# Another way of turning the third graph's normed x, and another order of work under the first graph's attention

## The chip, the core and the metric

The kernel runs on one core of a Trainium2 chip. The metric is the time of one execution on the device in microseconds (us), as the median of several runs. The core has five engines that run side by side, each in its own order of instructions: TensorE (PE, matrix products and transposes), VectorE (DVE), ScalarE (ACT), GpSimd (POOL) and SyncE (SP). SP and POOL issue the transfers (DMAs) of this kernel. An engine waits for another, or for a transfer, through semaphores. All numbers are float32.

## The reference, cut to what matters

There are 16 graphs (b) with 1024 nodes (n) and 256 channels (c), one adjacency matrix for all of them, and two layers. Each layer adds its result to x.

```python
# layer 0: graph attention
h = maximum(layernorm(x), 0)                  # (16, 1024, 256), "normed x"
fea = transpose(h, (0, 2, 1))
c_adj = mean(fea, axis=1)                     # mean over channels
diff = c_adj[:, None, :] - c_adj[:, :, None]
A = abs(abs(sigmoid(diff) - 0.5) - 0.5) * 2
Wg = adj * (A + A.transpose(0, 2, 1)) * 0.5   # weights of each graph
g = relu(einsum('bcn,bnm->bcm', fea, Wg) * para)
q = heads(transpose(g))                       # 4 heads of 64 channels
k, v = heads(h @ kv_w)
x = x + softmax(q k^T * scale) v
# layer 1: graph convolution with batch norms
h = maximum(layernorm(x), 0)
A_norm = adj + eye
deg = column sums + row sums - diagonal of A_norm
A_hat = A_norm * rsqrt(deg)[:, None] * rsqrt(deg)[None, :]
agg = einsum('nm,bmd->bnd', A_hat, h)
x = x + batchnorm(relu(batchnorm(agg @ W1.T + b1)) @ W2.T + b2)
```

## The kernel before, in words

**Steps and background.** `attention()` (L1240) goes through 16 steps for each graph: 2 pairs of heads, 2 halves of the queries, 4 groups of keys. In a step PE makes two tiles of scores (`scores`, L1071), ACT takes their exponentials (L1089), DVE adds these up (L1113), and PE multiplies the exponentials of the step before with the values (L1124). The scores live in two PSUM buffers (`ps_sc`), so the scores of a step start only when ACT has done the exponentials of the step before.

Between the steps lies other work, made by the generator `background(b)` (L964): it prepares the next graphs and finishes earlier ones. Each `yield` names a cost in us of PE's time. `attention` hands out pieces while the costs handed out are below the share that is due, `total * (step + 1) / 16`. A piece of cost 0 comes along with its neighbours. A piece that yields `TOP` runs at the top of the next step, ahead of the values' product. `weave(main, (start, side), ...)` takes one piece of each side after every piece of the main generator, from the `start`-th on. Each engine runs its instructions in the order in which this Python code issues them; nothing is rescheduled.

**What lies under the first graph's attention** (`background(0)`, L966 to L997):

- `transposed(1, (k,))` (L412) turns the second graph's normed x, one half of its channels at a time: 8 transposes on PE (L424) and 2 copies on ACT (L430) from PSUM into a tile `ht`. Keys and values need x turned in this way.
- `keys_values(1)` (L672): 4 pieces of keys (`pk`), 4 pieces of values (`pv`), each of 1.71.
- `plain_queries(1)` (L638): 16 pieces (`pg`), eight for each half of the nodes. The two sums of a half stay in two of the three PSUM banks of `bank()` until DVE has multiplied them with `para` (L663).
- `weighers[1]`, made by `weigh` (L477): 17 slots for eight weight tiles `w`. An even slot closes the tile before with a multiply-add on DVE (L495), which frees a block of `adj`, and lets ACT begin the next tile (L508); an odd slot is ACT's tanh (L516). A block of `adj` is loaded one tile ahead, through SP (L192).
- `Norm(2, True).all()` (L391): the third graph's norm in 8 pieces, on DVE, POOL and ACT (L368).
- `graph()` (L252): the build of combined adjacency blocks in DRAM, on POOL and POOL's queue.
- `degrees()` (L233): for each of eight slabs of `adj_t`, a load through SP (L226), a copy with a row sum on ACT (L241), and the diagonal on DVE (L243, L244). Load t + 2 is issued with slab t.
- `differences(2)` (L456): the third graph's channel sums are turned on DVE (L467), written to DRAM by four SP transfers (L469) and read back as a broadcast tile `cbc` (L473), SP waiting for the four in between.
- `transposed(2, ...)`, and the first 6 slots of the third graph's `weigh`.

**Shared buffers.** Blocks of `adj` and slabs of `adj_t` come from one pool of three buffers (tag `adj`), used in turn: a slab's load has to wait until the third last user of that pool is done. SP issues its transfers in one order, and a transfer that waits for a buffer holds up all that follow.

**The other way to turn x** is in use for the fourth graph on. `squares(b)` (L432): for each half of the channels DVE transposes the 32 x 32 squares of a 128 x 1024 tile into `sq` (L438; one buffer), and POOL's queue writes it to DRAM (L442). `gathered(b, k)` (L446) reads it back in four SP transfers (L452), which put the squares in their places in `ht`.

Of the kernel before, what the change touches and what calls it, by code (L numbers as in the profile page):

```python
# [23 lines left out]
def gnn_two_layers_kernel(  # L24
# [12 lines left out]
    nc = tc.nc  # L37
    B, N, C = x.shape
    H1 = w1_t.shape[1]
    NT = N // P  # L40
    CC = C // P
# [32 lines left out]
    hsq_d = [dram.tile([P, CC, N], F32, name=f"hsq_d{b}") for b in range(B)]  # L74
# [24 lines left out]
    def layers(shifted):  # L99
# [51 lines left out]
        def weave(main, *sides):  # L151

            for i, cost in enumerate(main):
                for start, side in sides:
                    if i >= start:
                        cost += next(side, 0.0)
                yield cost
            for _, side in sides:
                yield from side

        def double(slots):

            for _ in slots:
                next(slots, None)
                yield 0.0
# [244 lines left out]
        TOP = -1.0  # L410
# [21 lines left out]
        def squares(b):  # L432

            for k in range(CC):
                sq = p1.tile([P, N], F32, tag="sq", name=f"sq_{b}_{k}")
                nc.vector.transpose(  # L438
                    sq.rearrange("p (i t s) -> p i t s", i=NS, s=SQ),
                    hs["a", b][:, :, k * P : (k + 1) * P].rearrange("p t (i s) -> p i t s", s=SQ),  # L440
                )
                nc.gpsimd.dma_start(out=hsq_d[b][:, k], in_=sq)  # L442
                for _ in range(3):
                    yield 0.0

# [442 lines left out]
        def lately():  # L888

            while late:  # L890
                late.pop(0)()
                yield 0.0
# [71 lines left out]
        def background(b):  # L964

            if b == 0:  # L966
                differences(1)
                for k in range(CC):
                    yield TOP
                    transposed(1, (k,))  # L970
                    yield 1.0
                w, products, norm = weighers[1], keys_values(1), Norm(2, True).all()
                yield from weave(islice(products, 4), (0, double(islice(w, 8))))
                asked, build, sums = plain_queries(1), graph(), degrees()
                yield from weave(
                    islice(asked, 13),
                    (0, w),
                    (4, norm),
                    (5, islice(build, 8)),
                    (7, islice(sums, 6)),  # L980
                )
                differences(2)
                yield from weave(asked, (0, build), (0, sums))
                w = weighers[2]
                yield from islice(products, 1)
                yield from weave(islice(products, 2), (0, islice(w, 2)))
                yield TOP
                transposed(2, (0,))
                yield 1.0
                yield from weave(islice(products, 1), (0, islice(w, 1)))  # L990
                yield from islice(w, 1)
                yield TOP
                transposed(2, (1,))
                yield 1.0
                yield from islice(w, AHEAD - 4)
                yield from products
                return  # L997
            before = hidden(b - 1)
            gather = aggregate(b - 1)
            if b + 1 < B:  # L1000
                w, products, norm = weighers[b + 1], keys_values(b + 1), normed(b - 1)
                yield from weave(islice(products, 4), (0, islice(w, 4)))
                asked = queries(b + 1)
                yield from weave(islice(asked, 7), (0, double(w)))
                if b == 1:
                    load_later()
                yield from weave(asked, (2, islice(norm, 5)))
                if b + 2 < B:
                    load_x(b + 2, True)
                yield next(gather)  # L1010
                yield from weave(products, (0, norm))
            else:
                yield next(gather)
                yield from weave(endings.pop(), (2, normed(b - 1)))
            if b + 2 < B:
                yield from weave(gather, (0, summed(b + 2)), (1, lately()))
                yield from prepare(b + 2, before)
            elif b + 2 == B:

                yield from weave(gather, (1, lately()))  # L1020
                endings.append(before)
            else:
                yield from weave(gather, (1, lately()))
                yield from weave(before, (0, normed_last()))
# [215 lines left out]
        def attention():  # L1240

            units = [Unit(b, k, f) for b in range(B) for k in range(CC) for f in range(NH)]
            steps = [(u, g) for u in units for g in range(NG)]
            per_graph = CC * NH * NG
            before = None
            at_top, at_mid, at_end, adds = {}, {}, {}, {}
            bg, done, total, top = iter(()), 0.0, 0.0, False
            for s in range(len(steps) + 2):
                if s < len(steps):
                    unit, g = steps[s]  # L1250
                    b = unit.at[0]
                    if s % per_graph == 0:
                        run(bg)
                        top = False
                        bg, done = background(b), 0.0
                        total = (37.6 if b > 0 else 41.0) * (b + 1 < B) + 24.0 * (b > 0) + 6.0 * (b == 0)
                        total += 12.0 * (0 < b < B - 2) + 25.7 * (b == B - 1) + 3.0 * (b == 0)

                        total -= 10.3 * (b == B - 1)
                    made = scores(*unit.at, g)  # L1260
                    due = total * (s % per_graph + 1) / per_graph
                    if b == B - 1:
                        due -= 0.5 * min(s % per_graph + 1, (per_graph - 1 - s % per_graph) * 0.75)
                else:
                    due += 5.1
                for action in at_top.pop(s, ()):
                    action()
                if top:
                    done += advance(bg)
                    top = False  # L1270
                for action in at_mid.pop(s, ()):
                    action()
                if s in adds:
                    adds.pop(s)()
                if s < len(steps):
                    for pr in made:
                        unit.add(pr)
                if before is not None:
                    (last, g_last), prs = before
                    last.values(g_last, prs)  # L1280
                    if g_last == NG - 1:

                        if last.closes:
                            last.fold(0)
                            last.fold(1)
                            at_top.setdefault(s + 1, []).append(last.sums)
                            wait = 1
                        else:
                            for e in range(2):
                                at_end.setdefault(s + e, []).append(lambda u=last, e=e: u.fold(e))  # L1290
                            opens = last.by_squares and last.at[1:] == (0, 0)
                            wait = 6 if opens else 4
                            at_mid.setdefault(s + 3 + opens, []).append(last.sums)
                        if last.by_squares:
                            at_top.setdefault(s + 2, []).append(last.gather)
                        else:
                            at_top.setdefault(s + wait, []).append(last.finish)
                        adds[s + wait] = last.add_output
                while done < due and not top:
                    cost = advance(bg)  # L1300
                    if cost is None:
                        break
                    if cost == TOP:
                        top = True
                        break
                    done += cost
                for action in at_end.pop(s, ()):
                    action()
                before = (steps[s], made) if s < len(steps) else None
            run(bg)  # L1310

        with st:
            if shifted:
                for b in range(B):
# [13 lines left out]
                    norm = Norm(b, False)  # L1328
# [6 lines left out]
            else:  # L1335
# [7 lines left out]
                norm = Norm(0, True)  # L1343
# [11 lines left out]
                products = keys_values(0)  # L1355
# [357 lines left out]
```

## Time and profile before

| what | value |
| --- | --- |
| median of 3 runs | 2460.37 us (2460.0 to 2460.49) |
| the profiled execution's own time | 2460.34 us |
| its span in the trace | 2458.6 us |
| PE busy | 2412.4 us, 98% |
| DVE, ACT, POOL busy | 82%, 51%, 23% |
| PE transposes of the second and third graph (L424) | 32 |
| DVE transpose of a 128 x 1024 tile (L438) | 26 times, 1.236 us each |
| write of such a tile to DRAM (L442), issue to landing | 3.0 / 4.1 / 8.4 us (least, median, most) |

The profiled execution's time is 1.7 us more than its span, and 0.03 us below the median of the runs. Times in the trace count from the span's start. The first graph's attention runs from 54 to about 161 us; all that the change touches lies in it. "Idle before, releaser" tells how long an engine stood still before an instruction and what ended that. The end of a PE matmul is modelled; the starts are recorded.

### The profile page before, as it was taken

To read this page: it belongs to the slowest core of one execution; us is meant where nothing else is said; L and a number is where in the kernel's file an instruction comes from. 1 tells how busy PE (TensorE), PEld (TensorE's weight loads), DVE (VectorE), ACT (ScalarE), POOL (GpSimd) and SP (SyncE) were. 2 spreads that over 40 slices of the span, in tenths; PEclk is the share of its full clock that TensorE was granted. 3 is DMA by queue.
4 is the path that set the end of the run, shared out by engine and by line. 5 is a ranking of instruction groups with operands and counts; after the bars stand their busy time and mean duration, and the time that the engine had idled before them with its cause. 6 is when DMAs were issued, how large, how long until landed. Compare 5 with 4: busy or idle time off the path is not lost. (4 is left out here: it accounts for less than half of the span.)

```text
span 2458.6 us, 35932 instructions
## 1 busy us (share of the span) xinstructions
PE 2412.4 (98%) x13290; PEld 832.6 (34%) x13290; DVE 2003.9 (82%) x3103; ACT 1257.7 (51%) x1870; POOL 559.5 (23%) x645
## 2 busy tenths in 40 slices
PE   9999999999999999999999999999999999999994
PEld 4333333333333333333333333333333332334444
DVE  5678888988888888888898888888888878767775
ACT  7874554545464545445454546454454534335554
POOL 1381202111111212020211212121202103136652
PEclk9999999999999999999999999999999999999997
DMA  4675545363645554453536355544545353456559
GB/s 146 204 242 182 172 138 179 118 229 125 209 139 193 171 189 163 158 171 126 209 117 231 120 201 160 197 164 167 172 134 188 116 201 142 152 197 230 196 193 372
DMA packets 204553, 437.18 MB, mean 178 GB/s; under 512 B 21456, under 2 KB 96720, under 8 KB 200272
## 3 DMA queue, kind: packets, MB, share of 16 engines
q1 hardware_dynamic: 173328, 327.29, 39.7%
q0 software_dynamic: 31040, 107.50, 11.6%
q8 instruction: 107, 1.75, 0.3%
q14 instruction: 78, 0.64, 0.1%
HBM read 331.36 MB, written 103.35 MB: 177 GB/s over the span
## 5 line engine op out<-in xcount | busy, mean ns | idle before, releaser
L1089 ACT ACTIVATE p<-sc 128x1024 f32<-128x1024 f32 x512 | 495.4, 1020 | 649.5 <-PE sc L1081 649.5
L1113 DVE TENSOR_TENSOR acc<-acc,p 128x1024 f32<-128x1024 f32 x384 | 469.8, 1223 | 58.2 <-ACT p L1089 36.9
L1081 PE MATMUL sc<-q,k 64*64 64x512 f32 x4096 | 498.6, 602 | 0.5 <-ACT p L1089 0.5
L1124 PE MATMUL o<-p,v 128*64 128x512 f32 x2048 | 494.7, 604 | 0.0
L174 PE MATMUL pa<-aht,h_b 128*64 128x512 f32 x1536 | 346.0, 592 | 1.1 <-ACT h_b L368 1.1
L174 PE MATMUL pg<-w,x_h 128*64 128x512 f32 x1472 | 332.0, 592 | 0.0
L1081 PEld LDWEIGHTS sc<-q,k 64*64 64x64 f32 x4096 | 131.5, 132 | 336.4 <-issue 287.8
L1124 PEld LDWEIGHTS o<-p,v 128*64 128x64 f32 x2048 | 124.6, 136 | 297.7 <-issue 251.2
L1142 POOL DMA_DIRECT2D out_d<-os x58 | 32.9, 568 | 803.2 <-DVE os L1138 803.2
L495 DVE SCALAR_TENSOR_TENSOR w<-w,adj 128x1024 f32<-128x1024 f32 x128 | 164.9, 1288 | 46.1 <-ACT w L516 45.1
L174 PEld LDWEIGHTS pa<-aht,h_b 128*64 128x64 f32 x1536 | 110.1, 137 | 220.6 <-issue 207.8
L174 PEld LDWEIGHTS pg<-w,x_h 128*64 128x64 f32 x1472 | 105.7, 137 | 210.1 <-issue 198.4
L508 ACT ACTIVATE w<-cbc,csum 128x512 f32<-128x512 f32 x256 | 170.3, 716 | 0.0
L516 ACT ACTIVATE w<-w 128x1024 f32<-128x1024 f32 x128 | 135.6, 1059 | 2.5
L571 DVE TENSOR_TENSOR w<-w,w 128x1024 f32<-128x1024 f32 x112 | 134.6, 1232 | 1.5
L174 PE MATMUL pv<-kvw_f,ht 128*64 128x256 f32 x1024 | 116.1, 379 | 0.0
L174 PE MATMUL pk<-ht,kvw_f 128*64 128x512 f32 x512 | 115.2, 593 | 0.2 <-ACT ht L430 0.2
L174 PE MATMUL py<-at,w 128*64 128x512 f32 x464 | 112.6, 593 | 0.8 <-DVE at L729 0.7
L174 PE MATMUL py<-at,w1s 128*64 128x512 f32 x448 | 107.9, 595 | 0.0
L1453 ACT ACTIVATE yin_f<-yin_f,sm_f 128x512 f32<-128x512 f32 x128 | 93.5, 803 | 19.0 <-DMA yin_f<-y_d 17.0
L826 POOL DMA_DIRECT2D y_d<-y x112 | 61.6, 550 | 145.1 <-DVE y L846 75.8
L1160 DVE TENSOR_REDUCE part<-acc 128x16 f32<-128x512 f32 x128 | 87.8, 686 | 4.4
(197 smaller groups left out, 2968.6 us busy)
## 6 DMA issues: line engine op xcount, KB each, us to landing
aht<-aht_d SPq DMA_DIRECT2D x224, 512.0 KB
adj<-in_adj_dram SPq DMA_DIRECT2D x128, 512.0 KB
y_d<-y POOLq DMA_DIRECT2D x128, 256.0 KB, 3.0
yin_f<-y_d SPq DMA_DIRECT2D x32, 1024.0 KB
para<-in_para_dram SPq DMA_DIRECT2D x64, 256.0 KB
x_d<-x_x POOLq DMA_DIRECT2D x16, 1024.0 KB, 5.1
xo_f<-x_d SPq DMA_DIRECT2D x32, 512.0 KB
out_dram<-xo_f POOLq DMA_DIRECT2D x32, 512.0 KB, 11.1
```

The costliest lines, as they stand in the source:

```text
L174: nc.tensor.matmul(dst[r], left[:, r], right, start=start, stop=stop)
L495: nc.vector.scalar_tensor_tensor(w, w, 1.0, a, op0=ALU.add, op1=ALU.mult)
L508: nc.scalar.activation(w[:, t, :].rearrange("p (t q) -> p t q", q=P), cbc[:, q * NT // NH : (q + 1) * NT // NH], AF.Abs, bias=csum[:, th * ...
L516: nc.scalar.activation(made[i], made[i], AF.Tanh, scale=-0.5 / C)
L571: nc.vector.tensor_sub(block(i)[part], block(x)[part], block(y)[part])
L826: nc.gpsimd.dma_start(out=y1_d[i][:, j, :], in_=y)
L1081: nc.tensor.matmul(sc[part, e, :], ks[b][k][r, m * P + c * HW : m * P + (c + 1) * HW], qs[b][k][r, f * FB : (f + 1) * FB], start=True, sto ...
L1089: nc.scalar.activation(pr, sc, AF.Exp)
L1113: nc.vector.tensor_add(self.acc, self.acc, pr)
L1124: nc.tensor.matmul(self.o[r, :], vs[b][k][:, m, r], pr[:, e, :], start=(m == 0), stop=(m == NT - 1),)
L1160: nc.vector.tensor_reduce(self.part[:, e, :], acc.rearrange("p (c s) -> p c s", s=SQ), AX.X, ALU.add)
L1453: nc.scalar.activation(y, y, AF.Relu, bias=sh[:, j : j + 1], scale=scale[:, j : j + 1])
```

## The change: what it does

In `squares`, the third graph's tile (b == 2) is written to DRAM through SP's queue; the others stay on POOL's. In `background(0)`: the weight slots 0 and 1 come ahead of the keys, then all eight pieces of keys and values with one slot each (before: the four pieces of keys with two slots each). The queries come after them. The norm, the build and the degrees start 4 pieces earlier within the queries, which is the same place counted from the start. `differences(2)` comes after the eighth piece of the queries (before: after the thirteenth). The remaining eight pieces carry the third graph's `squares` and the first 4 of its weight slots. After the queries, `gathered` brings both halves of the turned x, in place of `transposed(2, ...)`. The total of costs to hand out goes from 50 to 48.

```diff
@@ -439,7 +439,8 @@
-                nc.gpsimd.dma_start(out=hsq_d[b][:, k], in_=sq)
+                queue_of = nc.sync if b == 2 else nc.gpsimd
+                queue_of.dma_start(out=hsq_d[b][:, k], in_=sq)
                 for _ in range(3):
                     yield 0.0
@@ -970,30 +971,20 @@
                 w, products, norm = weighers[1], keys_values(1), Norm(2, True).all()
-                yield from weave(islice(products, 4), (0, double(islice(w, 8))))
+                yield from islice(w, 2)
+                yield from weave(products, (0, islice(w, 8)))
                 asked, build, sums = plain_queries(1), graph(), degrees()
                 yield from weave(
-                    islice(asked, 13),
-                    (0, w),
-                    (4, norm),
-                    (5, islice(build, 8)),
-                    (7, islice(sums, 6)),
+                    islice(asked, 8), (0, w), (0, norm), (1, islice(build, 7)), (3, islice(sums, 5))
                 )
                 differences(2)
-                yield from weave(asked, (0, build), (0, sums))
                 w = weighers[2]
-                yield from islice(products, 1)
-                yield from weave(islice(products, 2), (0, islice(w, 2)))
-                yield TOP
-                transposed(2, (0,))
-                yield 1.0
-                yield from weave(islice(products, 1), (0, islice(w, 1)))
-                yield from islice(w, 1)
-                yield TOP
-                transposed(2, (1,))
-                yield 1.0
+                yield from weave(
+                    asked, (0, squares(2)), (0, build), (0, sums), (4, islice(w, 4))
+                )
+                for k in range(CC):
+                    gathered(2, k)
                 yield from islice(w, AHEAD - 4)
-                yield from products
                 return
@@ -1254,7 +1245,7 @@
-                        total += 12.0 * (0 < b < B - 2) + 25.7 * (b == B - 1) + 3.0 * (b == 0)
+                        total += 12.0 * (0 < b < B - 2) + 25.7 * (b == B - 1) + 1.0 * (b == 0)
```

## The prediction

> **What bounds the kernel now.** I read the page first: PE is busy nearly all the time.
>
> ```profile
> PE 2412.4 (98%) x13290; PEld 832.6 (34%) x13290; DVE 2003.9 (82%) x3103; ACT 1257.7 (51%) x1870; POOL 559.5 (23%) x645
> ```
>
> Then the table by stretches of 20 us, for where the change lies. The first numbers after the length are PE, PEld, DVE, ACT, POOL.
>
> ```profile
> 100.00:120.00 20.00, 20.00 (x122) 6.17 (x120) 16.41 (x33) 16.00 (x33) 19.18 (x25) 1.00 0.79 254
> 120.00:140.00 20.00, 20.00 (x128) 6.80 (x126) 15.55 (x27) 11.79 (x19) 16.76 (x20) 1.00 0.91 314
> 140.00:160.00 20.00, 20.00 (x150) 8.63 (x150) 14.53 (x15) 13.94 (x24) 18.30 (x23) 1.00 0.59 190
> ```
>
> PE has no gap here, so PE work removed is time gained, and every wait that reaches PE is time lost. The DMA share of 0.91 is the second thing to see: the transfers are near their limit from 120 to 140.
>
> Third, the timeline of PE around what is removed:
>
> ```profile
> 150.10 1.09 PE L424 MATMUL htp<-ident,x_h 128*128 128x128 f32 x8
> 151.13 1.94 PE L1124 MATMUL o<-p,v 128*64 128x512 f32 x8
> ...
> 156.60 1.09 PE L424 MATMUL htp<-ident,x_h 128*128 128x128 f32 x8
> 157.62 0.31 PE L1173 MATMUL sums<-part,same 128*64 128x32 f32 x4
> ```
>
> Eight transposes hold PE for 1.03 and 1.02 us (start to next start).
>
> Last, the timelines of ACT and of SP's queue, for the loads that share SP with the new transfers:
>
> ```profile
> 121.72 1.06 ACT L241 ACTIVATE at<-at 128x1024 f32<-128x1024 f32 x1 [0.43 <-DMA at<-in_adj_t_dram]
> ...
> 135.57 1.06 ACT L241 ACTIVATE at<-at 128x1024 f32<-128x1024 f32 x1 [3.08 <-DMA at<-in_adj_t_dram]
> ```
>
> ```profile
> 109.48 9.64 SPq L226 DMA_DIRECT2D at<-in_adj_t_dram  x5
> 123.89 1.35 SPq L469 DMA_DIRECT2D csum_d<-csumt  x4
> 127.76 0.34 SPq L473 DMA_DIRECT2D cbc<-csum_d  x1
> 128.21 0.81 SPq L226 DMA_DIRECT2D at<-in_adj_t_dram  x1
> ```
>
> ACT already waits for the loads of the degrees twice, 0.43 and 3.08 us. ACT has slack there, so PE doesn't feel it. The change moves just this.
>
> **What the Trainium skill says.** "DMA: Bandwidth & Descriptors", section "Queues, rings and completion order": each DMA engine consumes the descriptors of a ring in order. The trace agrees: the sixth slab's load (its single issue is at 116.72) reached ACT at 121.72, 5.0 us later; the eighth, issued at 128.21 right behind `cbc`, took 7.36 us. Same page, "Anatomy of one DMA" (for GpSimd's path): about 2 us are fixed, mostly the receipt after the last byte. The eighth slab's last packets start at 133.7, ACT at 135.57: 1.9 us. "Perfetto Trace Analysis", section "Tensor Engine Instruction": ACT and DVE are strict FIFO; so the two waits above hold up everything behind them on ACT. "VectorE: DVE Perf Modes", "The three transpose paths": DVE turns only 32 x 32 blocks, into SBUF, which is why a trip through DRAM is needed; L438 shows 1.236 us for it.
>
> **The change part by part.** The built order of instructions of both kernels shows what moves.
>
> *PE: -2.05 us.* 16 transposes go. Matmuls of keys, values and queries are the same, in another order. By itself that gives 2460.37 - 2.05 = 2458.3.
>
> *ACT and DVE.* Four copies L430 of 0.59 go from ACT (2.4 us); two squares of 1.24 come to DVE (2.5 us), which is 73 to 82% busy in these stretches. Neither bounds PE: hidden under PE's 20 of 20. Uncovered, the squares would cost at most 2.5.
>
> *Keys and values first, slots singly.* The first weight slot now waits on ACT for the second graph's `cbc` ahead of the copies of the keys; the packets of that broadcast (issue 62.75) end at 66, PE begins the keys at 66.0 and needs the first copy only before its fourth piece at 71.2. I cost it 0. Five pieces lie in step 2 as before. Adding up PE's pieces (1.77 a piece, 3.7 the products of a step, 0.6 the four transposes `ot`), the scores of steps 8 to 12 would start at 107.3, 115.05, 122.25, 129.4 and 135.0 without a wait.
>
> *First new wait, the third slab of `adj_t`.* Its load takes the buffer of the last `adj` block, freed by the last L495. Before, that multiply-add ended at 109.46, the load was issued at 109.48, and ACT came to it at 115.09: 5.6 us for a load of about 5. Now the weight slots lie 2 pieces later against the norm and the degrees, which keep their place, and L495 stands on DVE behind the second slab's diagonal and a `para` product. ACT in step 8: exponentials end at 110.4, copy of the output 4.45 after the scores (108.99 to 113.44 before) to 112.25, tanh 0.97, two relus 1.17, second slab 1.05: 115.5. DVE: diagonal 0.7, product 0.6, multiply-add 1.25: 118.1. Load 5.0: 123.1. ACT, done with the next relus at 116.7, stands still for 6.4 us. Behind it wait the exponentials of step 9: slab 1.05, first exponential 1.0, so 125.2. PE wants their buffer for the scores of step 10 at 122.25: **2.9 us lost**. DVE is late after this too (fold 1.4, two sums of about 1.3, product 0.7 after the exponentials): the bank for the other query sum comes about **0.7 us** late. With a load of 4 us, as an idle queue would give, the first loss is 1.9; it is 0 only for a load of 2.1.
>
> *Second new wait, the seventh slab.* Before, its load was issued at 118.79, ahead of `differences(2)`. Now SP issues, in order: four writes of sums, `cbc`, two `para`, the first square, the seventh slab, the eighth, the second square. SP stands at the writes until DVE has turned the sums, which need the last relu: after the first wait about 130.5. `cbc` follows 3.9 us later (123.87 to 127.76 before): 134.5. Ahead of and with the slab are `cbc` 0.5 MB, `para` twice 0.25, the square 0.5, the slab 0.5: four times 0.5 MB. In the trace `cbc` and the eighth slab begin 1.6 after the issue, take 2.1 us per 0.5 MB beside POOL's build, and 1.9 to be seen: 7.8 for two, as measured. Four take 1.6 + 8.4 + 1.9 = 11.9, or 9.7 where POOL's queue pauses (84 packets of 4 KB a us). The slab lands between 144.2 and 146.4. ACT is at it from 133.5. Behind it are the exponentials of step 11: 2.05 later, 146.3 to 148.5. PE comes to the scores of step 12 at 135.0 + 3.6 = 138.6: **7.7 to 9.9 us lost, 8.8 in the middle**. Without the first wait the same sum ends near 140 against 135.0, still some 4 to 5 us.
>
> *Squares and gathers on SP.* The second square needs the first one's write landed (one buffer): by then it is, since DVE waits for ACT. It comes about 6 us after the slab, its write 5 later. Three blocks of `adj`, the second write and both gathers are some 3 MB, at 0.22 MB a us 14 us plus landing: about 22 after the slab. PE reaches the third graph's keys 29 after it. Hidden with about 7 to spare. Later transfers on SP (`adj` for the third graph) wait for the same queue, with as much room. POOL's queue loses nothing and gains nothing before the second graph.
>
> *`total` 50 to 48.* It follows the two units of cost that go; the last piece of queries falls in step 13, two steps of attention alone remain. 0.
>
> Sum against the profiled execution: span 2458.6, plus 1.7 around it, -2.05 + 2.9 + 0.7 + 8.8 = +10.3: 2470.7. The same from the median of the runs. I say **2470.5**.
>
> **The rivals.**
>
> *No wait reaches PE: 2458.3, chance 0.17.* For it: ACT has been 3 us late at this place before, and the stretches show ACT busy only 12 to 16 of 20. Against: it needs the third slab 2.1 us after its issue and the seventh by 133.0, and every load seen there takes 5 and more. This is the one that ends not slower: it decides where the seventh slab lands 2.05 us before PE's step 12.
>
> *One of the two waits only: 2461 to 2465, chance 0.13.* The first alone gives 2458.3 + 3.6 = 2461.9, the second alone 2458.3 + 4.5 = 2462.8. A higher rate for SP when POOL is behind would do it.
>
> *The gathers come too late as well: 2475 to 2485, chance 0.08.* Each us beyond the spare 7 adds one. For it: 2 MB more at a DMA share of 0.9. Against: the build's traffic thins out after 145, where PE's delay also gives them time.
>
> *Both waits, as summed: chance 0.62*, 2466 to 2475 with the loads' bounds (1.9 and 6 at least, 5 and 11 at most).
>
> That the transposes don't go is no rival: the built order has none for the third graph.
>
> **How the numbers follow.** A change under 0.2% (4.9 us) is about what a measurement of this kernel can't tell from none. Slower: the summed case and the late gathers, less a little for the low end: 0.68. Within: the no-wait and one-wait cases: 0.30. Faster by 4.9 us would need more than twice the PE work that goes: 0.02. The range reaches down to the no-wait case and up to the summed one's top: 2458 to 2475.
>
> **What would show it.** PE without L424 on the third graph; PE idle before L1081 at about 122 and 139, released by ACT L1089; ACT idle before L241, for a load, some 6 and 11 us; L438 at about 131 and 150; no wait of the keys L174 for the gathers. I am wrong if L241 finds its slabs landed, or if PE shows waits elsewhere: for a weight tile (L495) in the queries, or for the gathers.

## The result, and the profile after

The changed kernel takes 2469.44 us in the median of 7 runs (2467.87 to 2471.36), the kernel before 2460.44 us in 7 runs beside it (2460.0 to 2461.24). The ratio is 1.0036, with a 95% interval of 1.0026 to 1.0046: slower by 0.36%. The forecast was 2470.5. The number was right, but in part by luck: one wait that had been forecast did not come, and two losses that had not been forecast came in its place.

The profiled execution of the changed kernel took 2471.36 us; its span is 2469.6 us, 11.0 more than before. It is the slowest of the seven, 1.9 us above their median, so the account that follows explains its own 11.0 and not the 9.0 between the medians. The busy times on the page hardly differ from those of before:

```profile
PE 2414.4 (98%) x13274; PEld 832.2 (34%) x13274; DVE 2007.5 (81%) x3105; ACT 1256.4 (51%) x1866; POOL 554.5 (22%) x645
```

There are 16 PE records fewer, yet PE is busy 2.0 us *longer*. That is the first sign that something besides waiting is at work. The table by stretches of 20 us shows where (after the length: busy us and count of PE, PEld, DVE, ACT, POOL; then the granted clock of PE, the DMA share, GB/s):

```profile
120.00:140.00 20.00, 15.18 (x88) 4.41 (x84) 13.78 (x19) 8.82 (x16) 14.25 (x20) 1.00 0.91 319
140.00:160.00 20.00, 15.66 (x76) 4.97 (x78) 13.55 (x19) 12.78 (x17) 16.27 (x20) 0.74 0.78 271
```

PE was busy for 20 of 20 us in both before. Now it is idle for 4.8 us of the first and 4.3 of the second, and in the second stretch the clock stands at 0.74. The timeline of PE shows what this is: one pause, with its idle time in square brackets.

```profile
133.29 1.89 PE L174 MATMUL pg<-w,x_h 128*64 128x512 f32 x8
144.34 3.69 PE L1072 MATMUL sc<-q,k 64*64 64x512 f32 x16 [9.16 <-ACT p L1080]
...
154.97 1.95 PE L1072 MATMUL sc<-q,k 64*64 64x512 f32 x16
```

The scores of step 12 wait 9.16 us for ACT's exponentials of step 11. Then they take 3.69 us in place of the 1.95 of any other step. From the scores of step 12 to those of step 13 it is 10.63 us, where the same instructions take 7.76 in a run without the pause (the last experiment below): 2.87 us more, after the wait. ACT's timeline gives the reason for the wait:

```profile
118.60 1.06 ACT L241 ACTIVATE at<-at 128x1024 f32<-128x1024 f32 x1 [0.53 <-DMA at<-in_adj_t_dram]
...
142.23 1.06 ACT L241 ACTIVATE at<-at 128x1024 f32<-128x1024 f32 x1 [11.22 <-DMA at<-in_adj_t_dram]
143.28 1.92 ACT L1080 ACTIVATE p<-sc 128x1024 f32<-128x1024 f32 x2
```

The seventh slab of `adj_t` reaches ACT at 142.23, after 11.22 us in which ACT does nothing; the exponentials of step 11 stand behind it. The third slab (118.60) waited 0.53 us, where 6.4 had been forecast. And the timeline of SP's queue shows what stood ahead of the seventh slab:

```profile
125.62 1.56 SPq L470 DMA_DIRECT2D csum_d<-csumt  x4
130.06 0.34 SPq L474 DMA_DIRECT2D cbc<-csum_d  x1
130.44 1.15 SPq L649 DMA_DIRECT2D para<-in_para_dram  x2
131.72 0.35 SPq L443 DMA_DIRECT2D hsq_d<-sq  x1
132.11 1.37 SPq L226 DMA_DIRECT2D at<-in_adj_t_dram  x2
```

The last line holds the seventh and the eighth slab; the seventh is issued at 132.11, 13.3 us later than before (118.79). From the issue of `cbc` to ACT's start on the slab it is 142.23 - 130.06 = 12.17 us; the prediction had 11.9 for four transfers of 0.5 MB.

Last, the table by stretches of 2 us, for the clock (third column from the end):

```profile
148.00:150.00 2.00, 2.00 (x12) 1.05 (x10) 1.97 (x4) 1.03 (x1) 2.00 (x4) 0.50 0.24 84
150.00:152.00 2.00, 2.00 (x12) 0.70 (x10) 1.97 (x3) 0.34 (x1) 1.98 (x3) 0.90 1.00 342
152.00:154.00 2.00, 2.00 (x12) 0.57 (x10) 1.97 (x4) 1.97 (x4) 1.92 (x3) 1.00 1.02 231
```

After the pause PE runs at exactly half the clock until about 150.4, and then at the full one. In the slow step it is ACT that waits for PE's scores, and not PE for ACT:

```profile
148.09 1.03 ACT L1080 ACTIVATE p<-sc 128x1024 f32<-128x1024 f32 x1 [0.68 <-PE sc L1072]
```

So the account of the profiled execution is: -2.05 for the transposes, +9.16 for the wait, +2.87 for the half clock, +0.7 at the end of the program (PE waits 1.87 us for DVE ahead of the last transposes `pt_f`, 1.13 before). The sum is +10.7; the span grew by 11.0. The last term need not come from the change: in the traces of the experiments below the same waits add up to anything from 0.35 to 1.8 us.

### The profile page after: what moved, and what is told of

It is laid out like the page before. It is cut to its first block, busy times and chain, and to the rows that moved or that the text cites. A ratio compares the mean times of both kernels' runs of the same rounds, so it can differ in the third digit from the quotient of the medians.

```text
span 2469.6 us, 35905 instructions
## 1 busy us (share of the span) xinstructions
PE 2414.4 (98%) x13274; PEld 832.2 (34%) x13274; DVE 2007.5 (81%) x3105; ACT 1256.4 (51%) x1866; POOL 554.5 (22%) x645
## 5 line engine op out<-in xcount | busy, mean ns | idle before, releaser
L496 DVE SCALAR_TENSOR_TENSOR w<-w,adj 128x1024 f32<-128x1024 f32 x128 | 165.6, 1294 | 44.2 <-ACT w L517 39.9
L1101 DVE TENSOR_TENSOR acc<-p,p 128x1024 f32<-128x1024 f32 x64 | 79.6, 1244 | 16.5 <-ACT p L1080 16.5
```

Of the source, the lines that this page charges most:

```text
L496: nc.vector.scalar_tensor_tensor(w, w, 1.0, a, op0=ALU.add, op1=ALU.mult)
L1101: nc.vector.tensor_add(self.acc, self.held, pr)
```

## The experiments

The theory at this point: the loss is made by the *order*, because the sums of the third graph (`differences(2)`) now come after the fifth piece of the degrees and so `cbc`, the two `para` and the first square stand on SP ahead of the seventh slab. Rivals: the way through DRAM itself costs the time (squares on DVE, writes and gathers), or the slow step after the pause is held-up work and not the clock.

The kernel before was timed beside each of these runs; its medians there are 2460.18 to 2460.33 us.

**1. The old transposes in the new order.** The changed order is kept; the squares and the gathers go, and the PE transposes come back.

```diff
-                    asked, (0, squares(2)), (0, build), (0, sums), (4, islice(w, 4))
+                    asked, (0, build), (0, sums), (4, islice(w, 4))
                 )
                 for k in range(CC):
-                    gathered(2, k)
+                    yield TOP
+                    transposed(2, (k,))
+                    yield 1.0
...
-                        total += ... + 1.0 * (b == 0)
+                        total += ... + 3.0 * (b == 0)
```

> The changed kernel's order of values, queries, norm and degrees, with the third graph's x turned by PE as in the kernel before (no squares, no trip through DRAM, total 50). Theory (order on SP): cbc and para still lie ahead of the seventh slab, only the square is gone, so some 7 us of wait remain and 2 us of transposes come back: 2467 to 2470. Rival (sheer traffic): 2 MB of transfers are gone, the wait falls to 4 or less, 2461 to 2465. Rival (the squares on DVE make it late): no wait, 2460.4 as the kernel before.

Measured: 2469.49 us (6 runs), ratio 1.0036, 95% 1.0023 to 1.0048. The whole loss is there without one square or gather. PE's timeline has the same pause at the same step (two more of 0.64 and 0.43 come before it):

```profile
146.00 3.55 PE L1074 MATMUL sc<-q,k 64*64 64x512 f32 x16 [7.86 <-ACT p L1082]
```

`cbc` to the slab took 10.96 us here, with three transfers of 0.5 MB in place of four. It began later, at 132.93, so that the pause is nearly as long. The order makes the loss without the new way of turning x.

**2. The seventh slab first.** In `degrees`, the load of the seventh slab is issued with the fourth slab's work and not with the fifth's, which puts it ahead of the channel sums on SP.

```diff
-                if t + 2 < NT:
+                if t + 2 < NT and t != 4:
                     ahead.append(load_adj_t(t + 2, "at"))
+                if t == 3:
+                    ahead.append(load_adj_t(t + 3, "at"))
```

> The changed kernel, with the load of the seventh slab issued one piece earlier, ahead of the third graph's channel sums; nothing else moves. Theory (order on SP): the seventh slab lands by about 130, and the 9.2 us at the scores of step 12 are gone; the eighth slab, still behind cbc, para and the first square, lands near 142 and costs 0 to 2 us at the scores of step 13. Time 2458 to 2461. Rival (sheer traffic) and rival (DVE is late): the bytes and DVE's work are the same, the wait stays within 2 us of 9.2, time 2467 to 2470.

Measured: 2462.74 us (20 runs, 2460.26 to 2465.11), ratio 1.0010, 95% 1.0003 to 1.0017; the span of the profiled execution is 2459.4. The pause of 9.16 is gone. What is left in this execution is a smaller one, a step later, from the eighth slab, which still stands behind `cbc`, `para` and the square:

```profile
145.08 2.00 PE L1074 MATMUL sc<-q,k 64*64 64x512 f32 x16 [1.77 <-ACT p L1082]
```

Moving one load by one slot takes back 6.7 of the 9.0 us between the two medians. The bytes and DVE's work are the same, so the place of this load on SP is what makes the pause of 9.16. The time itself was missed: the lowest runs lie within the 2458 to 2461 that was expected, the median 1.7 above it. The traced execution (2461.29) is one of the faster ones, and what the median run waits for was not seen.

**3. One more transfer ahead of the slab.** The first square is written twice (the second time into the first graph's place in DRAM).

```diff
                 queue_of.dma_start(out=hsq_d[b][:, k], in_=sq)
+                if b == 2 and k == 0:
+                    nc.sync.dma_start(out=hsq_d[0][:, k], in_=sq)
```

> The changed kernel with one more write of 0.5 MB on SP, of the first square into an unused part of DRAM, between the square's write and the seventh slab's load. Theory (order on SP): the wait grows by 2.1 us to about 11.3, the time by 2.1 to about 2471.5. Rival (the wait is for DVE's squares, or for ACT itself): no change, 2469.4. How much more than the wait itself the time grows tells whether PE's clock falls further after a longer pause.

Measured: 2471.17 us (4 runs), 1.7 above the changed kernel's median. The time was met, but the wait was not: 11.3 had been expected, and the pause of the profiled execution is 9.44, only 0.3 more than in the changed kernel, since `cbc` was issued 1.1 us earlier there (128.97). That execution is even 0.5 us shorter in its span than the changed kernel's (2469.1 against 2469.6), so the 1.7 between the medians is in neither trace. What the trace does show is the way from `cbc` to the slab, 13.45 us, 1.3 more. With the other runs this gives the price of what stands in the way, from the issue of `cbc` to ACT's start on the slab:

| transfers of 0.5 MB, `cbc` and the slab included | us |
| --- | --- |
| 2 (before, eighth slab) | 7.8 |
| 3 (squares on POOL's queue; transposes) | 9.8; 11.0 |
| 4 (changed kernel; slab first, eighth slab) | 12.2; 11.2 |
| 5 (this run) | 13.5 |

By the two ends of the table it is (13.45 - 7.8) / 3 = 1.9 us for each 0.5 MB. The lines with two values scatter by 1.0 to 1.2 us, so this is a mean and no fixed price.

**4. The squares through POOL's queue.** One word is undone, so that SP carries one transfer of 0.5 MB less ahead of the slab.

```diff
-                queue_of = nc.sync if b == 2 else nc.gpsimd
+                queue_of = nc.gpsimd
```

> The changed kernel with one edit undone: the third graph's squares go to DRAM through POOL's queue. Theory (order on SP): the seventh slab is late because 0.5 MB each of cbc, para and the first square lie ahead of it in SP's ring, 2.1 us for each 0.5 MB. One of the three is gone, so PE's wait at the scores of step 12 falls from 9.2 to about 7 us, and the time by about 2 us to 2467. Rival (sheer traffic): the same bytes move at the same time through the other queue, so the slab is as late as before, 9.2 us and 2469.4. Rival (DVE is late with the squares): the same as well.

Measured: 2480.18 us (4 runs), ratio 1.0080, 95% 1.0063 to 1.0097. The time was missed by far, though the part that had been worked out came out: the pause at step 12 fell to 6.87. There is a second one now:

```profile
142.43 3.69 PE L1072 MATMUL sc<-q,k 64*64 64x512 f32 x16 [6.87 <-ACT p L1080]
...
173.01 3.69 PE L1072 MATMUL sc<-q,k 64*64 64x512 f32 x16 [9.66 <-ACT p L1080]
```

DVE's timeline and POOL's show where it comes from (the second fence is of POOL):

```profile
160.69 1.25 DVE L438 STREAM_TRANSPOSE sq<-x_h 128x1024 f32<-128x1024 f32 x1 [14.57 <-DMA hsq_d<-sq]
```

```profile
156.60 0.55 POOL L443 DMA_DIRECT2D hsq_d<-sq  x1
```

The first square was ready at 127.0, but POOL, deep in the build, issued its write only at 156.60. `sq` has one buffer, so DVE stood 14.57 us before the second square. ACT then waited 13.66 us for DVE's query product behind it, and PE for ACT. The queue that the change chose for this tile is thus worth 10.7 us in this order. What counted here was less what stood ahead in bytes than when the issuing engine came to it.

**5. The squares in the order of before.** Now the other half alone: the order of the kernel before, with squares, SP's queue and gathers in place of the transposes. The lines are marked against the kernel before.

```diff
-                yield from weave(asked, (0, build), (0, sums))
+                turn = squares(2)
+                yield from weave(asked, (0, build), (0, sums), (0, islice(turn, 3)))
...
-                yield TOP
-                transposed(2, (0,))
...
+                for k in range(CC):
+                    gathered(2, k)
+                yield from weave(products, (0, islice(w, 2)))
```

> The order of the kernel before (keys, queries, then values), with only the turning changed: squares on DVE and SP's queue in the last queries and the values' first piece, gathers after the third piece of values, total 48. Theory (order on SP): the eighth slab lies behind cbc alone, as before, and the squares come behind it, so no slab is late for PE; the 2.05 us of transposes are gained: 2458.4 on this scale (before 2460.4), PE without a wait over 1 us from 60 to 240. Rival (the trip through DRAM itself costs PE): the keys wait for the gathers, or DVE for the square's buffer, and the time is at or above 2460.4.

Measured: 2466.67 us (7 runs), ratio 1.0025, 95% 1.0014 to 1.0037. This expectation failed: in the old order the way through DRAM costs 6.3 us. PE's timeline, and then DVE's:

```profile
160.67 0.43 PE L1169 MATMUL sums<-part,same 128*64 128x32 f32 x4 [3.22 <-DVE part L1156]
```

```profile
158.05 1.22 DVE L496 SCALAR_TENSOR_TENSOR w<-w,adj 128x1024 f32<-128x1024 f32 x1 [4.48 <-DMA adj<-in_adj_dram]
```

A weight tile's multiply-add waits 4.48 us for its block of `adj`, DVE's sums behind it come late, and PE waits 3.22 us and then works at half the clock (the product with the values behind it takes 3.66 us in place of 1.94). SP's queue shows why the block is late:

```profile
134.69 14.70 SPq L443 DMA_DIRECT2D hsq_d<-sq  x2
149.43 1.36 SPq L192 DMA_DIRECT2D adj<-in_adj_dram  x2
```

SP stands at the write of the second square until 149.06, for DVE makes that square only at 147.80. The blocks of `adj` for the third graph's weights stand behind it and are issued at 149.43 and 150.29; the kernel before issued its first two at 129.53 and 130.60. So the two halves of the change are no sum: a square that comes late holds up what SP has to issue behind it. Whether the squares could be placed early in the old order as well was not tested.

**6 to 8. How far the channel sums must go back.** If the slabs must stand ahead of the sums, it should be enough to hold `differences(2)` back. Three versions differ only in that. First, one query piece, one piece of the build and one of the degrees more ahead of the sums (the number of pieces of the degrees that the kernel before had):

```diff
-                    islice(asked, 8), (0, w), (0, norm), (1, islice(build, 7)), (3, islice(sums, 5))
+                    islice(asked, 9), (0, w), (0, norm), (1, islice(build, 8)), (3, islice(sums, 6))
```

> After, with one more query piece, one more step of the build and one more of the degrees ahead of the channel sums (9, 8, 6 in place of 8, 7, 5): only the seventh slab's load passes to the front of the sums, the eighth stays behind cbc and the first square. Theory: no wait for the seventh slab, one of 1 to 2 us at step 13 for the eighth (about 11 us after cbc), no lowered clock: 2459 to 2462. Rival (one piece is too little, the sums are later too and the wait moves to the eighth slab in full): a wait of 4 to 9 us at step 13, 2464 to 2470.

Measured: 2467.50 us (6 runs), ratio 1.0030. The rival came in. The seventh slab cost ACT only 0.95 us. But one piece later, the turn of the channel sums stands on DVE behind the additions of a step's exponentials (130.30 to 133.18). The sums are issued at 133.33 and `cbc` at 135.64, 5.6 us later than in the changed kernel, and the eighth slab, still behind `cbc` and the square, inherits the wait. ACT's timeline:

```profile
145.28 1.06 ACT L241 ACTIVATE at<-at 128x1024 f32<-128x1024 f32 x1 [9.59 <-DMA at<-in_adj_t_dram]
```

PE pauses 4.05 us at step 13, twice more after it (0.5 and 1.6), and half the clock follows the first. Second, two pieces, with both slabs ahead of the sums and the squares left where they were:

```diff
+                turn = squares(2)
+                yield from weave(islice(asked, 2), (0, islice(turn, 2)), (0, islice(build, 2)), (0, islice(sums, 2)))
                 differences(2)
                 w = weighers[2]
                 yield from weave(
-                    asked, (0, squares(2)), (0, build), (0, sums), (4, islice(w, 4))
+                    asked, (0, turn), (0, build), (0, sums), (3, islice(w, 3))
                 )
```

> The changed kernel with the third graph's channel sums two pieces later (after the tenth piece of the queries), so that the loads of the seventh and the eighth slab are issued ahead of the sums and cbc; of the third graph's weight slots one fewer is done ahead. Theory (order on SP): both slabs land in time (para and the first square still lie ahead of the seventh: at most 1 us of wait), and the time is the kernel before less 2.05: 2458.4 to 2459.5. Rival (sheer traffic, or DVE late with the squares): at least half of the 9.2 us stays, 2463 or more. A new wait would be ACT's for cbc at the first weight slot of the third graph.

Measured: 2460.07 us (13 runs, 2458.28 to 2464.29), ratio 0.9999, 95% 0.9991 to 1.0008. The loss of the changed kernel is gone, though the median lies 0.6 above the 2458.4 to 2459.5 that was expected. PE's timeline has one short pause left under the first graph's attention, from the seventh slab, issued right behind the square's write:

```profile
136.58 2.00 PE L1074 MATMUL sc<-q,k 64*64 64x512 f32 x16 [1.43 <-ACT p L1082]
```

Third, as the second, but with the squares behind the sums as well (the first `weave` without `turn`, the second with `(1, squares(2))`):

> After, with the channel sums after the tenth query piece and the squares behind them: both late slabs, then the sums and cbc, are on SP ahead of the first square's write. Theory (what costs is what stands on SP ahead of a slab): ACT finds the seventh slab landed or waits under 2 us, no PE wait over 0.5 us at steps 12 and 13, the sixteen transposes are gained whole: 2458.3 to 2459.5, below both kernels. Rival (the squares are now too late): the first square comes some 13 us later than in the changed kernel, the gathers with it, and the keys of the third graph (start near 172) or the weight tiles wait for SP: 2461 to 2466, with a PE wait after 155 in place of the one at step 12.

Measured: 2465.51 us (21 runs, 2460.33 to 2468.52), ratio 1.0019, 95% 1.0013 to 1.0026. The pause at step 12 is gone, and the rival came in all the same. PE's timeline at the keys of the third graph:

```profile
167.44 6.21 PE L174 MATMUL pk<-ht,kvw_f 128*64 128x512 f32 x20 [3.75 <-DMA ht<-hsq_d]
```

Its second square was written at 151.05. In the changed kernel that was 148.85, but there PE was 12 us late itself and reached the keys at 173.99. Here it reaches them at 162.4, and the gathers do not.

**9 and 10. The clock after a pause.** To tell the clock from held-up work, PE is kept busy in the pause: matmuls of zeros are added into the query sum that is open just ahead of the scores of step 12. First 32 of them, then 16.

```diff
+                        if not shifted and (b, q, th, k) == (1, 1, 1, 1):
+                            for n in range(32):          # the second time: range(16)
+                                nc.tensor.matmul(pgs[k][n % 2 * HW : (n % 2 + 1) * HW], zeros,
+                                    h[:, 0:2, :].rearrange("p t c -> p (t c)"), start=False, stop=False)
```

> After, with 32 matmuls of zeros (0.24 us each, 7.6 us) added into the query sum just ahead of the scores of step 12, where PE waits 9.2 us. They change no value and wait for nothing. Theory (after a pause TensorE runs at a lower clock): the wait left is about 1.6 us, the scores of step 12 take 1.95 us in place of 3.69, from step 12 to step 13 it is 7.8 us in place of 10.6, and the time falls by 2.9 to 2466.5, though work was added. Rival (the slow step comes from work held up by ACT, not from the clock): step 12 to step 13 stays at 10.6 us and the time at 2469.4.

Measured: 2472.24 us (5 runs). The time was missed, because the filling was sized wrong: a matmul of 128 x 512 shows as two records of 0.217 us and not as one, so that 32 of them took 13.90 us, 4.7 more than the pause. But the step behind it went as it should if the clock is the cause. PE's timeline:

```profile
135.37 13.90 PE L666 MATMUL pg<-x_h,zeros 128*64 128x512 f32 x64
149.21 1.95 PE L1083 MATMUL sc<-q,k 64*64 64x512 f32 x16
...
156.97 1.95 PE L1083 MATMUL sc<-q,k 64*64 64x512 f32 x16
```

PE came to the scores 4.87 us later than in the changed kernel, and to step 13 only 2.0 us later: 7.76 us for the step and not 10.63. This run alone doesn't rule out held-up work, since ACT had 4.87 us more to catch up. Then with half the number:

> As the kernel with 32 matmuls of zeros, with 16: those took 0.434 us each (13.90 us), twice what was taken for them, so that PE came to the scores of step 12 4.9 us later than without them, and still got to step 13 only 2.0 us later. 16 take 6.9 us and leave a wait of about 2.2. Theory (a lowered clock after the pause): scores of step 12 at 144.3, 1.95 us long, step 13 7.8 us later, 2466.5. Rival (no gain from the clock, only other work moved): step 13 10.6 us after step 12, 2469.4.

Measured: 2467.17 us (8 runs, 2465.38 to 2468.75), 2.3 below the changed kernel, with 7 us of work *added*. Its profiled execution (2465.38, the lowest) shows

```profile
135.39 7.04 PE L666 MATMUL pg<-x_h,zeros 128*64 128x512 f32 x32
142.37 2.00 PE L1083 MATMUL sc<-q,k 64*64 64x512 f32 x16
```

Step 13 begins at 150.19: the step takes 7.8 us, and no wait is left in this execution, as its slab came 2 us earlier than in the changed kernel's. PE comes to the scores just as ACT lets go of their buffer, as in the changed kernel, so held-up work would show here. It doesn't, and the granted clock stays at 1.00. The span fits: 2458.6 - 2.05 + 7.04 = 2463.6, as measured. The slow step is the clock.

**11. The slab ahead of the square.** The second of the three versions above, with the sides of its first `weave` in another order, so that within one query piece the slab's load comes ahead of the square's write:

```diff
-                yield from weave(islice(asked, 2), (0, islice(turn, 2)), (0, islice(build, 2)), (0, islice(sums, 2)))
+                yield from weave(islice(asked, 2), (0, islice(build, 2)), (0, islice(sums, 2)), (0, islice(turn, 2)))
```

> As the kernel with the channel sums after the tenth query piece, but within a piece the degrees' load comes before the square: the seventh slab's load passes the first square's write on SP, nothing else moves on that queue. Theory: ACT finds the seventh slab after about 1.4 us in place of 3.3, PE waits under 0.3 us at step 12 in place of 1.4, the gathers stay in time: 2458.3 to 2459.3, below both kernels. Rival (the wait passes on to the eighth slab, which now stands behind the square): 1 to 2 us at step 13, 2460 as before.

Measured: 2458.86 us (13 runs, 2458.17 to 2460.09) beside 2460.24 (20 runs, 2459.90 to 2460.72) before. The ratio is 0.9995, and its interval of 0.9986 to 1.0003 holds 1. So it beats the changed kernel by 10.6 us; against the kernel before the median is 1.4 us lower, which the interval does not separate from nothing. PE's timeline and SP's:

```profile
135.11 1.95 PE L1074 MATMUL sc<-q,k 64*64 64x512 f32 x16
...
142.87 1.52 PE L1074 MATMUL sc<-q,k 64*64 64x512 f32 x12
```

```profile
125.44 0.88 SPq L226 DMA_DIRECT2D at<-in_adj_t_dram  x1
129.47 0.33 SPq L443 DMA_DIRECT2D hsq_d<-sq  x1
129.89 0.68 SPq L226 DMA_DIRECT2D at<-in_adj_t_dram  x1
134.63 1.31 SPq L470 DMA_DIRECT2D csum_d<-csumt  x4
139.24 0.34 SPq L474 DMA_DIRECT2D cbc<-csum_d  x1
```

No scores wait over 0.5 us, and step 12 takes its 7.76 (the last group is cut by the edge of the window). The span of this execution is 2457.9; with nothing but the transposes gone it would be 2456.55. Of the 1.35 us between, 0.7 is a wait of the second graph's value pieces `pv` for DVE (L606); the cause of the rest is open.

## Why the prediction was right, and where it was wrong

| term | forecast | measured |
| --- | --- | --- |
| sixteen transposes | -2.05 | -2.05 |
| first new wait, third slab | +2.9 | 0 |
| query bank late after it | +0.7 | 0 |
| second new wait, seventh slab | +8.8 | +9.16 |
| half clock after the pause | not named | +2.87 |
| end of the program | not named | +0.7 |
| sum | +10.3 | +10.7 of 11.0 |

**The step that failed is "First new wait, the third slab".** It had the third slab's load wait for the buffer that the last multiply-add L495 frees, on the ground that the pool's three buffers are used in turn, as the description of the kernel has it. In the kernel before the third slab did wait for that multiply-add (its end 109.46, the issue 109.48). In the changed kernel the trace doesn't show a turn. DVE's timeline and SP's queue:

```profile
112.62 0.28 DVE L243 TENSOR_TENSOR db<-at,ident 128x128 f32<-128x128 f32 x1
118.38 1.22 DVE L496 SCALAR_TENSOR_TENSOR w<-w,adj 128x1024 f32<-128x1024 f32 x1
```

```profile
112.92 0.33 SPq L226 DMA_DIRECT2D at<-in_adj_t_dram  x1
119.62 0.33 SPq L226 DMA_DIRECT2D at<-in_adj_t_dram  x1
```

SP issued the third slab at 112.92, as soon as the first slab's diagonal had been read on DVE (L243, until 112.90). The multiply-add in question (L496 now) ended at 119.60, and the *fifth* slab was issued at 119.62. One thing differs between the two kernels: on DVE the multiply-add now comes after the first two diagonals, and before it came ahead of them. Handing out the buffer whose last reader comes first in that order would give both; this was not tested. The forecast had taken the turn for a rule. ACT thus waited 0.53 us, and PE nothing.

**Of the cases, the one that came is "one of the two waits only".** It had a chance of 0.13, against 0.62 for both waits, and was priced at 2461 to 2465 (second wait alone: 2462.8), which is short by two errors. One is its own sum, "Without the first wait the same sum ends near 140 against 135.0, still some 4 to 5 us". The writes of the sums were issued at 125.6 in place of 130.5, so the forecast's own terms, taken 4.9 earlier, put the slab at 139.3 to 141.5, the end of the exponentials 2.05 later and the loss at 6.35 to 8.55. The forecast gives no working for its "near 140"; it would fit a sum that stops at the slab and counts no exponentials, but that is a guess. Measured were 142.23 and 9.16: `cbc` came 4.4 after the first write and not 3.9, and the slab 12.2 after `cbc` and not 11.9. The other error is the clock, +2.87, which no case had. In the sum that was forecast, the first wait with what follows it (3.6), which did not come, stood in for the two terms that were missing (2.87 and 0.7). That the sum came so near is luck.

**What held.** The mechanism of the second wait, its place (scores of step 12, released by ACT's exponentials behind the copy of the seventh slab), the transfers ahead of it and their price of about 2 us each. Experiments 1 and 2 show the place on SP, the table under experiment 3 the price. *Keys and values first* cost nothing: up to step 11 the scores start within 0.15 us of the forecast (107.41, 115.17, 122.35, 129.53). *Squares and gathers on SP* were hidden, with no wait at the keys at 173.99. But this rested on PE being late: experiment 8 takes the pause away and makes the squares late, and the gathers miss the keys by 3.75 us.

**The rival of no wait (2458.3)** is what experiment 11 comes near to. It was right on what it takes, the seventh slab landed by 133: ACT begins it at 132.56 there.

## What to carry to other kernels

A reorder that takes work from the busiest engine can still move a load behind others on its queue. List what the queue issues ahead of each load that an in-order engine waits for, and follow it to the last of them: holding the sums back by one piece only passed the wait on to the next slab. Price a pause of TensorE by its length plus what the half clock after it costs; here that was 1.5 to 2.9 us more for every pause over 3 us. A transfer that is hidden behind a pause is hidden only while that pause is there.

## What the runs showed of the hardware

After a pause of PE of over 3 us the granted clock is 0.50, and it comes back to 1.00 by itself under work. A mean between the two appears only in stretches in which the clock changes. The Trainium skill says so: "TensorE: Matmul & The Clock Gate", section "What's actually happening", has two states, full and half, with half after an idle window of about 3.4 us. The pauses under the first graph's attention fit it roughly: after 1.43 and 1.77 us the clock stayed full, after 3.22, 3.75, 4.05, 6.87, 7.86, 9.16, 9.44 and 9.66 us it was halved. The window is not exact here: in the pause of 3.22 us (experiment 5) the clock fell at 159.9, about 2.5 us after PE's last work, and in that of 3.75 us (experiment 8) at 168.2, 0.7 us after PE had begun to work again. The loss (the work behind the pause against the same work undisturbed) was, in the same order, 2.9, 1.8, 1.5, 2.2, 1.6, 2.9, 2.2 and 2.2 us: it does not grow with the pause.

Twice the loss is the time that PE works at half clock, 3.0 to 5.8 us. The same page gives about 3.4 us of activity for the way back; the measured times lie from a little below that to well above it. From fall to return the clock stood at half for 3.4 us (experiments 6 and 8), 6.8 (experiments 1 and 5, and the first pause of 4) or 10.2 (140.15 to 150.39 in the changed kernel; experiment 3; the second pause of 4). These are one, two and three times the same length. That half clock follows a pause of this length was on that page, and the prediction had not used it; what it costs in this kernel the runs here show.

The versions in which PE waits for a transfer also scatter more. The 7 runs of the kernel before lie within 1.3 us of each other. The changed kernel spreads over 3.5 us, the version with only the seventh slab ahead over 4.9, the one with the late squares over 8.2, though the order of instructions is the same from run to run.
